# Product 1 of a two-level fast matrix product made joint over two pairs of tiles

## The chip, the core and the metric

The kernel runs on one core of a Trainium2 chip. The metric is the device time of one execution in microseconds; before the change it is 1103.38 us, the median of three runs. The engines are named PE (TensorE), DVE (VectorE), ACT (ScalarE), POOL (GpSimd) and SP (SyncE, which here issues all DMAs). Each has its own instruction queue and works it off in order.

## What is computed

The reference has a cross attention to a short memory and then a linear layer with a mixture of low-rank experts, each behind a layer norm and each added to x:

```python
x = x + xattn(layernorm(x), ctx_2048, mask)        # x: (8, 1024, 1024) float32, ctx: (8, 64, 1024)
x = x + ffn(layernorm(x), W, lora_A, lora_B, router_w)

# xattn: scores = h @ ctx.T / sqrt(D), masked, softmax, readout = attn @ ctx
# ffn:   base = h @ W.T                            # 1024 x 1024, all in float32
#        logits = h @ router_w.T ; top 2 of 8 experts, their softmax weights
#        expert_out = sum over experts of w_e * (h @ A_e.T) @ B_e.T * 2
```

## The kernel before

The 8192 rows are 64 tiles of 128 rows. Two tiles make a *pair* (tile r = 0 and r = 1), numbered u = 0 to 31; two pairs u and v = u + 1 make a *quad*. `first()` treats pairs 0 and 1, then `quad(u)` runs for u = 2, 4, ..., 30. Everything is laid out by hand: within `tc.manual_schedule` every engine executes its instructions in the order in which the Python code issues them, and an instruction waits on semaphores for what it reads and for what it overwrites. While a quad's linear layer runs, the attention of later pairs is threaded in between: in `quad(u)`, n and m (u + 2, u + 3) are the next quad's pairs, f and g (u + 4, u + 5) those of the one behind it.

**The linear layer.** For each pair, `h` (normalised rows) is turned on DVE into two halves of the contraction: `hA` (k = 0 to 3) and `hB` (k = 4 to 7), each 128 x 512 a tile (`rt_turn_tile`, line 557). To get there the rows go out to DRAM (`hd`) and come back blocked (`hs`). The 2 x 2 blocks (two tiles, two halves) are multiplied by the 2 x 2 blocks of W with Winograd's form of Strassen's scheme: seven products in place of eight. POOL makes the sums of the left side: `rt_sums` (line 629) makes s1, s2, s4 of a pair in three instructions of 128 x 512, and `rt_sum_3` (line 640) makes s3 in the place of `has[u][:, 1]`. Weights' sums `t1` to `t4` are made once in `first()`.

Products 2 to 7 are done *jointly* for the two pairs of a quad. `joint(i, u)` (line 788) takes the two pairs' 128-column operands as the rows of one more 2 x 2 scheme, so seven blocks of two 128 x 128 x 256 matmuls give what two products of four 128 x 128 x 512 matmuls gave. `joint_sums(i, u)` (line 774) makes that level's left sums on POOL in four instructions of 128 x 256; `quarter_sums` (line 680) made the weights' once. Inside `joint`, `to_x` brings quarter results from PSUM to where they are summed; block 5 (`block(chain, s2, q2, False)`, line 849) goes on accumulating in a bank whose first use must have been read, so PE waits there for that `to_x`. `hooks` give work of other stages that is issued behind step 1 to 7.

**Product 1** is not joint before. `product(u, 1)` (line 710) multiplies `has[u][:, 0]` by w11 into a bank `ch`; `one_add` (line 735) adds it to three of the pair's four output blocks, and much later `product(u, 8)` adds the low-rank term to the same bank and `product_add(u, 8)` takes it to the fourth. Product 6 goes to three of the output blocks as well: `joint(6, u)` puts it into `t_of(u)`, the place of `has[u][:, 0]` (free by then), and `six_add` (line 744) adds it to x on POOL.

**The start of a quad** (lines 1104 to 1216). On PE: product 1 of u, the last low-rank matmul of joint 4 of the quad before (`pending.pop()()`), the logits and low-rank matmuls `pa` of u (`rt_low_rank_tile`), product 1 of v with the turn `sc` of m's scores in it, `pa` of v with the turn `trw` of u's weighted low-rank part (`rt_turn_low_rank`), product 8, then readouts `ro`, scores `sct`, readouts, and joint 6. `trw` needs `rt_top(u)` (line 585): the top two experts' choice, some twenty short DVE instructions on the logits, of which several have both inputs in SBUF. On DVE `rt_top(u)` stands between the turn of v's tile 0 and that of v's tile 1; behind it come the turns `xT` of f and g for the attention, `att_divide`, `att_add(n)`, `rt_top(v)`, `att_add(m)`. On POOL: `rt_sums(u)` (already within joint 4 before, line 1295), `rt_sum_3(u)`, `rt_sums(v)`, `joint_sums(6)`, `rt_sum_3(v)`. On ACT: `x_sums(m)` of the attention's layer norm, which waits for `load_xt`, and the copy `axl` of the logits out of PSUM, with which `rt_top` begins. The order of the stages behind is joint 6, 2, 7, 3, 5, 4.

Of the kernel before, what the change touches and what calls it, by code (L numbers as in the profile page):

```python
# [14 lines left out]
ALU = mybir.AluOpType  # L15
# [9 lines left out]
def kernel(  # L25
# [520 lines left out]
    def hb_tile(u: int, r: int):  # L546
        if r == 0:
            h_tiles(u)
        t = turned.tile([P, KH, P], F32, tag="hB", name=f"hB_{u}_{r}", bufs=5)
        hbs[u].append(t)  # L550
        return t

    def rt_turn_pe(u: int, r: int):
        hb = hb_tile(u, r)
# [14 lines left out]
        for r in range(2):  # L569
            rt_low_rank_tile(u, r)  # L570

    def rt_low_rank_tile(u: int, r: int, midway=None):
        if r == 0:
            pas[u] = ps_rt.tile([P, 2, ER + E], F32, tag="rt", name=f"pa_{u}")
        pa = pas[u]
        for k in range(KD):
            h = has[u][:, r, k, :] if k < KH else hbs[u][r][:, k - KH, :]
            mm(pa[:, r, :], h, art_sb[:, k, :], start=(k == 0), stop=(k == KD - 1))  # L578
            if midway and k == KH:
                midway()  # L580
        if r == 1:
            axls[u] = small.tile([P, 2, ER + E], F32, tag="axl", name=f"axl_{u}", bufs=1)
            nc.scalar.copy(axls[u], pas.pop(u))

    def rt_top(u: int):

# [67 lines left out]
                by(o[:, k, :], x1[:, k, :], x2[:, k, :], op)  # L654


    quarters = {}

    def quarter(w, i: int, j: int):
        return w[:, i * HK : (i + 1) * HK, j * HH : (j + 1) * HH]  # L660
# [1 line left out]
    def quarter_sums_steps(name: str, w):  # L662

        by = nc.gpsimd.tensor_tensor
        b11, b12, b21, b22 = [quarter(w, i, j) for i in (0, 1) for j in (0, 1)]
        q2, q3, q4 = [
            const.tile([P, HK, HH], F32, name=f"{name}_{i}") for i in (2, 3, 4)
        ]
# [95 lines left out]
    def operand(i: int, p: int):  # L764

        if i in (2, 4):
            return hbs[p][i // 2 - 1]
        if i == 6:
            return sss[p]
        return {3: sms[p][:, 1], 5: sms[p][:, 0], 7: has[p][:, 1]}[i]  # L770
# [17 lines left out]
    def joint(i: int, u: int, hooks, final: bool = False, aside: bool = False):  # L788

# [11 lines left out]
        name = {2: "w21", 3: "w22", 4: "t4", 5: "t1", 6: "t2", 7: "t3"}[i]  # L801
        b11, b21, b22, q1, q2, q3, q4 = quarters[name]
        lower, upper = bank_of(f"jl{i}_{u}"), bank_of(f"ju{i}_{u}")
        p2, p5, p4, chain = [b[:, k * HH : (k + 1) * HH] for b in (upper, lower) for k in (0, 1)]

        def to_x(p, src, first: int, n: int):
            if i == 6:
                t = t_of(p)[:, first : first + n]
                if n == HH and (p == u and first == 0 or aside):
                    nc.scalar.copy(t, src)  # L810
# [85 lines left out]
    def first():  # L896
# [193 lines left out]

    pending = []

    def quad(u: int):

        v, n, m, f, g = [u + i for i in range(1, 6)]
# [5 lines left out]
        early = more and u == 2  # L1101
        late = more and u > 2

        product(u, 1, (lambda: att_sc(n)) if early else None, 1)
        if late:
            x_sums(m, (0,) if far else (0, 1))
            if not far:
                x_squares(m)
        if new_mem:
            mask_bias(b)  # L1110
        pending.pop()()
        if early:
            att_divide(n)
        one_add(u)
        rt_low_rank_tile(u, 0)
        if early:
            att_turn_p(n)
        rt_low_rank_tile(u, 1)
        if early:
            att_turn(m)  # L1120
        rt_turn_tile(v, 0)
        rt_top(u)
        rt_turn_tile(v, 1)
        if late:
            if far:
                x_sums(m, (1,))
                x_squares(m)
            x_root(m)
            product(v, 1, lambda: att_sc(m))
            if far:  # L1130
                att_turn_tile(f, 0)
                load_xs(g, (1,))
                att_turn_tile(f, 1)
            att_rstd(m)
            att_shift(m)
        rt_sum_3(u)
        rt_sums(v)
        if early:
            load_xs(f)
        elif far:  # L1140
            load_xt(f)
        if late:
            rt_low_rank_tile(v, 0)
            rt_turn_low_rank(u, bank_of(f"trw_{u}")[:, : 2 * P])
            att_exp(m)
            one_add(v, (0,))
        elif early:
            att_readout(n)
            att_scores(m)
            load_xs(g, (0,))  # L1150
            product(
                v, 1,
                {0: lambda: att_sc(m), 1: lambda: rt_turn_low_rank(u), 2: lambda: product(u, 8)},
            )
            att_rstd(m)
            att_exp(m)
            att_add(n)
            att_divide(m)
            f_sums(n)
            att_turn_tile(f, 0)  # L1160
            load_xs(g, (1,))
            load_xt(f)
            rt_low_rank_tile(v, 0)
            att_turn_tile(f, 1)
        else:
            product(v, 1)
            rt_low_rank_tile(v, 0)
            rt_turn_low_rank(u, bank_of(f"trw_{u}")[:, : 2 * P])
        if far:
            att_turn_tile(g, 0)  # L1170
        if late:
            att_divide(m)
        if far:
            att_turn_tile(g, 1)
        if late and not far:
            att_readout(n)
            att_add(n)
        rt_low_rank_tile(v, 1)
        if early or late and not far:
            att_turn_p(m, True)  # L1180
        if not early:
            product(u, 8)
        joint_sums(6, u)
        rt_sum_3(v)
        if late and far:
            att_readout(n)
            att_turn_p(m, True)
        product_add(u, 8)
        if late and far:
            att_add(n)  # L1190
# [5 lines left out]
        if far or not more:  # L1196
            rt_top(v)
        if more:
            att_readout(m)
        if late and not far:  # L1200
            att_add_tile(m, 0)
            rt_top(v)
        if late:
            f_sums(n)
        if new_mem:
            load_mem(b)
        if late and not far:
            att_add_tile(m, 1)
        elif more:
            att_add(m)  # L1210
        left_over = []
        if late:
            one_add(v, (1,))
            left_over.append(lambda: one_add(v, (2,)))
        else:
            one_add(v)

        hooks = {5: left_over, 7: []}
# [12 lines left out]
        def six():  # L1231
# [5 lines left out]
        if far:  # L1237
            x_stats(f)
            hooks[3].append(lambda: att_sc(f))
        if more:  # L1240
            hooks[3].append(lambda: f_rows(n))
        hooks[5] = []
# [49 lines left out]

        hooks = {1: [rows_0]}
        if more:
            hooks[3] = [lambda: rt_sums(n)]
        end_4 = joint(4, u, hooks, not more)

        def last():
            end_4()
# [55 lines left out]
```

## Time and profile before

| | |
|---|---|
| median of 3 runs | 1103.38 us (1103.31 to 1104.0) |
| profiled execution, span | 1101.5 us |
| granted TensorE clock | 1.00 |
| ACT busy | 556.2 us, 50% |
| matmul time of a whole product's piece, 128 x 512, mean of one | 593 ns (248 of them) |
| matmul time of a joint's piece, 128 x 256, mean of one | 385 ns (`ju` from w and s_j, 360) |
| DVE add from PSUM, 128 x 512 | 678 ns (124) |
| POOL sum, 128 x 512 / 128 x 256 | 1280 ns (31) / 731 ns (45) |
| DMA, mean over the span | 158 GB/s, 50.3% of 16 engines |

Each `mm` of float32 stands as two MATMUL instructions in the trace. A row of the timeline has the start in the span, the duration, the engine, the line, the operation with its tiles, and how many like it were joined; in square brackets stands the idle time before it and what ended it. Durations of matmuls include the drain of the array, which overlaps with the next one.

### The profile page before, as it was taken

What the parts mean: (1) busy time and instruction counts of PE and PEld (TensorE: products, weight loads), DVE (VectorE), ACT (ScalarE), POOL (GpSimd) and SP (SyncE); (2) the same over time, 40 slices, a digit from 0 to 9 for tenths busy, and PEclk for the clock granted to TensorE, in tenths of its full rate; (3) what the DMA queues carried; (4) which work ended last, traced back from release to release, by engine and by line L of the source; (5) the groups of instructions that cost most, each with busy time, mean ns of one, the idle gap of its engine ahead of it and who ended that gap; (6) DMA issues with size and microseconds to landing.
All of it is one profiled execution on the core that took longest, in us unless ns stands there. A gap on an engine that the chain in (4) does not pass through costs nothing.

```text
span 1101.5 us, 17562 instructions
## 1 busy us (share of the span) xinstructions
PE 1090.6 (99%) x5864; PEld 846.6 (77%) x5864; DVE 819.8 (74%) x2069; ACT 556.2 (50%) x1063; POOL 567.1 (51%) x629
## 2 busy tenths in 40 slices
PE   8999999999999999999999999999999999999998
PEld 6555787887878788787787878878787787877877
DVE  6666977769777687867869778687777778667665
ACT  4577363727539173573726638174472735636010
POOL 0079563635647265373644646356372644647372
PEclk9999999999999999999999999999999999999999
DMA  9857446363474625646265473635636355432301
GB/s 229 212 181 218 137 154 217 100 200 125 153 230 131 211 82 193 197 148 199 101 196 152 153 230 100 195 118 190 203 135 193 108 203 147 153 115 91 139 1 77
DMA packets 104921, 174.01 MB, mean 158 GB/s; under 512 B 12928, under 2 KB 77440, under 8 KB 104832
## 3 DMA queue, kind: packets, MB, share of 16 engines
q1 hardware_dynamic: 104832, 172.90, 50.3%
q8 instruction: 47, 0.77, 0.3%
q14 instruction: 42, 0.34, 0.1%
HBM read 107.84 MB, written 65.01 MB: 157 GB/s over the span
## 4 chain that ended last, share of the span: by engine, by line
PE 95%; DVE 2%; POOL 1%; ACT 1%; DMA 1%; SPq 0%; issue 0%; DVEq 0%; ACTq 0%; POOLq 0%
PE jl L703 28%; PE ju L703 21%; PE pa L578 10%; PE ch L703 9%; PE ro L480 5%; PE sct L412 5%; PE ju L695 4%; PE jl L695 3%; PE plain L703 3%; PE ch L695 2%; PE j L703 1%; DVE xT L89 1%; PE trw L621 1%; DMA xs<-in_x_dram 1%; PE ptp L466 1%; SPq L83 0%
## 5 line engine op out<-in xcount | busy, mean ns | idle before, releaser
L818 DVE TENSOR_TENSOR xt<-jl,xt 128x256 f32<-128x256 f32 x421 | 191.6, 485 | 139.6 <-PE jl L703 90.8
L818 DVE TENSOR_TENSOR xt<-ju,xt 128x256 f32<-128x256 f32 (+1 forms) x210 | 110.7, 551 | 56.2 <-PE ju L703 52.6
L635 POOL TENSOR_TENSOR s<-hA,hB 128x512 f32<-128x512 f32 x31 | 39.7, 1280 | 208.4 <-PE jl L703 92.9
L747 POOL TENSOR_TENSOR xt<-xt,hA 128x512 f32<-128x512 f32 x90 | 111.4, 1275 | 29.1 <-DVE hA L814 29.1
L195 ACT ACTIVATE junk<-xt 128x1024 uint8<-128x1024 f32 x60 | 63.2, 1053 | 123.6 <-DMA xt<-in_x_dram 123.1
L703 PE MATMUL ch<-w,hA 128*128 128x512 f32 x248 | 113.7, 593 | 0.0
L642 POOL TENSOR_TENSOR hA<-hA 128x512 f32<-128x512 f32 x31 | 39.6, 1277 | 139.8 <-PE pa L578 139.8
L703 PE MATMUL ju<-w,s_j 128*128 128x256 f32 x360 | 94.7, 385 | 0.2
L703 PE MATMUL ju<-t,s_j 128*128 128x256 f32 x360 | 92.7, 380 | 1.4 <-ACT hA L810 0.9
L692 DVE TENSOR_TENSOR xt<-ch,xt 128x512 f32<-128x512 f32 x124 | 81.3, 678 | 9.6 <-PE ch L703 4.5
L296 ACT ACTIVATE h<-xt,of_f 128x1024 f32<-128x1024 f32 x60 | 71.2, 1232 | 22.9 <-DVE of_f L292 14.1
L692 DVE TENSOR_TENSOR xt<-ro,xt 128x512 f32<-128x512 f32 x128 | 79.6, 676 | 3.7 <-PE ro L480 3.7
L703 PEld LDWEIGHTS ju<-t,s_j 128*128 128x128 f32 x360 | 66.2, 190 | 18.1 <-issue 5.3
L703 PEld LDWEIGHTS ch<-w,hA 128*128 128x128 f32 x248 | 44.7, 190 | 42.7 <-issue 41.8
L703 PE MATMUL jl<-t,s 128*128 128x256 f32 x300 | 76.0, 384 | 0.0
L703 PEld LDWEIGHTS ju<-w,s_j 128*128 128x128 f32 x360 | 63.9, 190 | 15.7 <-issue 6.8
L89 DVE STREAM_TRANSPOSE xT<-xs 128x1024 f32<-128x1024 f32 x60 | 73.6, 1229 | 0.6
L578 PEld LDWEIGHTS pa<-art_sb,hA 128*128 128x128 f32 x512 | 66.3, 190 | 9.8 <-issue 8.6
L578 PE MATMUL pa<-art_sb,hA 128*128 128x136 f32 x512 | 70.0, 280 | 0.0
L204 ACT ACTIVATE junk<-xt,of_x 128x1024 uint8<-128x1024 f32 x60 | 68.9, 1149 | 2.0
L578 PE MATMUL pa<-art_sb,hB 128*128 128x136 f32 x512 | 69.8, 279 | 0.0
L253 ACT ACTIVATE junk<-xt,of_f 128x1024 uint8<-128x1024 f32 x60 | 69.0, 1149 | 1.5
(202 smaller groups left out, 2425.0 us busy)
## 6 DMA issues: line engine op xcount, KB each, us to landing
xt<-in_x_dram SPq DMA_DIRECT2D x64, 512.0 KB, 4.8
out_dram<-xt SPq DMA_DIRECT2D x62, 512.0 KB, 3.0
xs<-in_x_dram SPq DMA_DIRECT2D x240, 128.0 KB, 4.1
hd<-h SPq DMA_DIRECT2D x60, 512.0 KB, 2.7
hs<-hd SPq DMA_DIRECT2D x240, 128.0 KB, 3.0
mem<-in_ctx_dram SPq DMA_DIRECT2D x16, 256.0 KB, 3.6
w<-in_w_t_dram SPq DMA_DIRECT2D x16, 256.0 KB, 10.0
ms<-in_ctx_dram SPq DMA_DIRECT2D x28, 64.0 KB, 2.0
```

Source lines behind the costliest of these rows:

```text
L89: nc.vector.transpose(dst.rearrange("p k (t i) -> p t k i", i=NB), src.rearrange("p t (k i) -> p t k i", i=NB),)
L195: nc.scalar.activation(nowhere, xts[u][r], AF.Identity, accum_out=sm[:, r, :])
L204: nc.scalar.activation(nowhere, xts[u][r], AF.Square, bias=nm[:, r, :], accum_out=ss[:, r, :],)
L253: nc.scalar.activation(nowhere, xts[u][r], AF.Square, bias=nm[:, r, :], accum_out=ss[:, r, :])
L296: nc.scalar.activation(h, xts[u][r], AF.Identity, bias=nmr[:, r, :], scale=rstd[:, r, :])
L412: mm(sct[r * M : (r + 1) * M, :], mt[:, k, :], x_ts[u][r][:, k, :], start=(k == 0), stop=(k == KD - 1),)
L578: mm(pa[:, r, :], h, art_sb[:, k, :], start=(k == 0), stop=(k == KD - 1))
L692: tt(xc, bank, xc, ALU.add)
L695: mm(bank, axwts[u][:, r, :], lb_sb[:, c0 : c0 + n], start=alone, stop=True, skip_group_check=True)
L703: mm(bank, a[:, k, :], w[:, k, :], start=(start and k == 0), stop=(k == n - 1), skip_group_check=True)
L747: nc.gpsimd.tensor_tensor(xc, xc, t_of(u), ALU.add)
L818: tt(xc, src, xc, ALU.add)
```

## The change

From the third quad (u = 4) on, product 1 is done by `joint(1, u)` too, behind the logits of both pairs. Its four quarter results go into `t_of(u)`, which is the place of its own left operand `has[u][:, 0]`; joint 6 then adds to what is there. All sums that read `has[u][:, 0]` come before the first copy into that place. `zero_add` adds product 1 alone to block (0, 0) on POOL before joint 6, and `six_add` later adds both to the other three. The low-rank term of block (1, 1) gets a bank of its own (`lora_alone`). The weights' quarter sums of w11 share one SBUF place with those of t1: both sets are written to DRAM once, and each quad loads w11's (`load_pieces` in joint 4, step 1, of the quad before) and t1's (in joint 2, step 3). In `first()`, `quarter_sums` and `keep_pieces` of w11 stand behind `plain(1, 0, 0)`, `keep_pieces` of t1 behind `t1_two()`. The places of `hB` are now assigned by hand, so that the fifth is spare for joint 1's s3. Quad 2 keeps the old order (`quad_start`).

```diff
+    def shared_pieces(name: str):
+        kept[name, "tile"] = sums.tile([P, 3, HK, HH], F32, tag="q", name=f"q_{name}")
+        return [kept[name, "tile"][:, i] for i in range(3)]
+    def keep_pieces(name: str):
+        kept[name] = dram.tile([P, 3, HK, HH], F32, tag=f"q_{name}", name=f"qd_{name}", bufs=1)
+        nc.sync.dma_start(out=kept[name], in_=kept[name, "tile"])
+    def load_pieces(name: str):
+        quarters[name] = *quarters[name][:4], *shared_pieces(name)
+        nc.sync.dma_start(out=kept[name, "tile"], in_=kept[name])
...
+    def zero_add(u: int):
+        xc = xts[u][0][:, :HB]
+        nc.gpsimd.tensor_tensor(xc, xc, t_of(u), ALU.add)
+
+    def lora_alone(u: int):
+        bank = bank_of(f"lo_{u}")
+        lora(u, bank, 1, HB, HB, True)
+        pps[u] = None, bank
...
         s3 = lo[:, :HK]
+        if i == 1:
+            s3 = turned.tile(
+                [P, KH, P], F32, tag=f"hB{spare_place(u)}", name=f"s3_{u}", bufs=1
+            )[:, :HK]
...
         def to_x(p, src, first: int, n: int):
-            if i == 6:
+            if i in (1, 6):
                 t = t_of(p)[:, first : first + n]
-                if n == HH and (p == u and first == 0 or aside):
+                if fresh and n == HH and p == u and first == (HH if i == 1 else 0):
                     nc.scalar.copy(t, src)
-                elif n == HH:
+                elif fresh and n == HH:
                     nc.vector.tensor_copy(t, src)
                 else:
                     tt(t, src, t, ALU.add)
...
+        quarter_sums("w11", w11)
+        keep_pieces("w11")
...
+        keep_pieces("t1")
...
+    def quad_joint_start(u: int):
...
+        if new_mem:
+            mask_bias(f // PPB)
+        rt_sums(u)
+        rt_low_rank_tile(u, 0)
+        rt_turn_tile(v, 1)
+        rt_sums(v)
+        pending.pop()()
+        if more:
+            x_sums(m, (0,))
+        rt_low_rank_tile(u, 1)
+        rt_top(u)
+        if more:
+            x_sums(m, (1,))
+            x_squares(m)
+        if far:
+            att_turn_tile(f, 0)
+            load_xs(g, (1,))
+            att_turn_tile(f, 1)
+            load_xt(f)
+        pa_v = bank_of(f"pa_{v}")
+        rt_low_rank_tile(v, 0, pa_v, False)
+        rt_low_rank_tile(v, 1, pa_v, False)
+        rt_sum_3(u)
+        rt_sum_3(v)
+        joint_sums(6, u)
+
+        hooks = {}
+        if more:
+            hooks[1] = [lambda: att_sc(m)]
+        def low_rank():
+            rt_turn_low_rank(u)
+            rt_low_rank_copy(v)
+            if more:
+                x_root(m)
+        def shift():
+            att_rstd(m)
+            att_shift(m)
+        hooks[2] = [low_rank]
+        if more:
+            hooks[4] = [shift]
+        end_1 = joint(1, u, hooks, fresh=True)
+        if more:
+            att_exp(m)
+        end_1()
+        for p in (u, v):
+            zero_add(p)
+        lora_alone(u)
+        if more:
+            att_divide(m)
+        if far:
+            att_turn_tile(g, 0)
+            att_turn_tile(g, 1)
+        if more:
+            att_readout(n)
+            att_turn_p(m, True)
+        product_add(u, 8)
+        if more:
+            att_add(n)
...
-        end_6 = joint(6, u, hooks, aside=not more)
+        end_6 = joint(6, u, hooks, fresh=not as_joint)
...
         def low_v():
-            product(v, 8)
+            if as_joint:
+                lora_alone(v)
+            else:
+                product(v, 8)
             product_add(v, 8)
...
+        if as_joint:
+            hooks[3].append(lambda: load_pieces("t1"))
...
         def rows_0():
+            if more:
+                load_pieces("w11")
             end_5()
...
         if more:
-            hooks[3] = [lambda: rt_sums(n)]
+            hooks[5] = [lambda: rt_turn_tile(m, 0)]
         end_4 = joint(4, u, hooks, not more)
+        if more:
+            joint_sums(1, n)
```

The quads from u = 4 on call `quad_joint_start(u)` and no longer issue `product(u, 1)`, `product(v, 1)`, `one_add` of either, or `rt_sums` of the next pair in joint 4. `quad_start` of quad 2 also makes `quarter_sum("w11")`, one POOL instruction, ahead of `joint_sums(6, 2)`.

More of the change, by code (lines that the diff above doesn't have):

```diff
@@ L548, in hb_tile, with place_of, spare_place @@
             h_tiles(u)
-        t = turned.tile([P, KH, P], F32, tag="hB", name=f"hB_{u}_{r}", bufs=5)
+        t = turned.tile(
+            [P, KH, P], F32, tag=f"hB{place_of(u, r)}", name=f"hB_{u}_{r}", bufs=1
+        )
         hbs[u].append(t)
         return t
+    places = {(u, r): (2 * u + r) % 5 for u in range(4) for r in range(2)}
+    def place_of(u: int, r: int):
+        if (u, r) not in places:
+            a, b, c, d = [places[p, k] for p in (u // 2 * 2 - 2, u // 2 * 2 - 1) for k in (0, 1)]
+            w = u // 2 * 2
+            places.update({(w, 0): a, (w, 1): c, (w + 1, 0): b, (w + 1, 1): d})
+        return places[u, r]
+    def spare_place(u: int):
+        used = {places[p, k] for p in (u, u + 1) for k in (0, 1)}
+        return ({0, 1, 2, 3, 4} - used).pop()
     def rt_turn_pe(u: int, r: int):
@@ L570, in rt_low_rank, with rt_low_rank_tile @@
             rt_low_rank_tile(u, r)
-    def rt_low_rank_tile(u: int, r: int, midway=None):
-        if r == 0:
+    def rt_low_rank_tile(u: int, r: int, bank=None, copy: bool = True):
+        if r == 0 and bank is not None:
+            pas[u] = bank[:, : 2 * (ER + E)].rearrange("p (r c) -> p r c", r=2)
+        elif r == 0:
             pas[u] = ps_rt.tile([P, 2, ER + E], F32, tag="rt", name=f"pa_{u}")
@@ L578, in rt_low_rank_tile, with rt_low_rank_copy @@
             mm(pa[:, r, :], h, art_sb[:, k, :], start=(k == 0), stop=(k == KD - 1))
[L579 to L583, printed above, removed]
+        if r == 1 and copy:
+            rt_low_rank_copy(u)
+    def rt_low_rank_copy(u: int):
+        axls[u] = small.tile([P, 2, ER + E], F32, tag="axl", name=f"axl_{u}", bufs=1)
+        nc.scalar.copy(axls[u], pas.pop(u))
     def rt_top(u: int):
@@ L654, in weight_sums @@
                 by(o[:, k, :], x1[:, k, :], x2[:, k, :], op)
-    quarters = {}
+    quarters, kept = {}, {}
+    SHARED = ("w11", "t1")
+    def shared_pieces(name: str):
[7 more added lines that the diff above has]
+        nc.sync.dma_start(out=kept[name, "tile"], in_=kept[name])
     def quarter(w, i: int, j: int):
@@ L665, in quarter_sums_steps @@
         b11, b12, b21, b22 = [quarter(w, i, j) for i in (0, 1) for j in (0, 1)]
-        q2, q3, q4 = [
-            const.tile([P, HK, HH], F32, name=f"{name}_{i}") for i in (2, 3, 4)
-        ]
+        if name in SHARED:
+            pieces = shared_pieces(name)
+        else:
+            pieces = [const.tile([P, HK, HH], F32, name=f"{name}_{i}") for i in (2, 3, 4)]
+        q2, q3, q4 = pieces
         quarters[name] = b11, b21, b22, b12, q2, q3, q4
@@ L769, in operand @@
             return sss[p]
-        return {3: sms[p][:, 1], 5: sms[p][:, 0], 7: has[p][:, 1]}[i]
+        if i in (1, 7):
+            return has[p][:, i // 7]
+        return {3: sms[p][:, 1], 5: sms[p][:, 0]}[i]
     jss = {}
@@ L786, in joint_sums, with joint @@
         jss[i] = s1, s2, s3, s4
-    def joint(i: int, u: int, hooks, final: bool = False, aside: bool = False):
+    def joint(i: int, u: int, hooks, final: bool = False, fresh: bool = False):
         v = u + 1
@@ L800, in joint @@
         s1, s2, s3, s4 = jss.pop(i)
-        name = {2: "w21", 3: "w22", 4: "t4", 5: "t1", 6: "t2", 7: "t3"}[i]
+        name = {1: "w11", 2: "w21", 3: "w22", 4: "t4", 5: "t1", 6: "t2", 7: "t3"}[i]
         b11, b21, b22, q1, q2, q3, q4 = quarters[name]
@@ L1091, with quad_start @@
     pending = []
+    def quad_start(u: int):
+        v, n, m, f, g = [u + i for i in range(1, 6)]
+        more, far = n < NP, f < NP
+        new_mem = far and f % PPB == 0
+        product(u, 1, lambda: att_sc(n), 1)
+        if new_mem:
+            mask_bias(f // PPB)
+        pending.pop()()
+        att_divide(n)
+        one_add(u)
+        rt_low_rank_tile(u, 0)
+        att_turn_p(n)
+        rt_low_rank_tile(u, 1)
+        att_turn(m)
+        rt_turn_tile(v, 0)
+        rt_top(u)
+        rt_turn_tile(v, 1)
+        rt_sum_3(u)
+        rt_sums(v)
+        load_xs(f)
+        att_readout(n)
+        att_scores(m)
+        load_xs(g, (0,))
+        product(
+            v, 1,
+            {0: lambda: att_sc(m), 1: lambda: rt_turn_low_rank(u), 2: lambda: product(u, 8)},
+        )
+        att_rstd(m)
+        att_exp(m)
+        att_add(n)
+        att_divide(m)
+        f_sums(n)
+        att_turn_tile(f, 0)
+        load_xs(g, (1,))
+        load_xt(f)
+        rt_low_rank_tile(v, 0)
+        att_turn_tile(f, 1)
+        att_turn_tile(g, 0)
+        att_turn_tile(g, 1)
+        rt_low_rank_tile(v, 1)
+        att_turn_p(m, True)
+        quarter_sum("w11")
+        joint_sums(6, u)
+        rt_sum_3(v)
+        product_add(u, 8)
@@ new lines, in quad_joint_start @@
+    def quad_joint_start(u: int):
+        v, n, m, f, g = [u + i for i in range(1, 6)]
+        more, far = n < NP, f < NP
+        new_mem = far and f % PPB == 0
+        next_mem = f + 2 < NP and (f + 2) % PPB == 0
+        if new_mem:
+            mask_bias(f // PPB)
+        rt_sums(u)
+        rt_low_rank_tile(u, 0)
+        rt_turn_tile(v, 1)
+        rt_sums(v)
+        pending.pop()()
+        if more:
+            x_sums(m, (0,))
+        rt_low_rank_tile(u, 1)
+        rt_top(u)
+        if more:
+            x_sums(m, (1,))
+            x_squares(m)
+        if far:
+            att_turn_tile(f, 0)
+            load_xs(g, (1,))
+            att_turn_tile(f, 1)
+            load_xt(f)
+        pa_v = bank_of(f"pa_{v}")
+        rt_low_rank_tile(v, 0, pa_v, False)
+        rt_low_rank_tile(v, 1, pa_v, False)
+        rt_sum_3(u)
+        rt_sum_3(v)
+        joint_sums(6, u)
+        hooks = {}
[7 more added lines that the diff above has]
+        def shift():
+            att_rstd(m)
+            att_shift(m)
[4 more added lines that the diff above has]
+        if more:
+            att_exp(m)
+        end_1()
[3 more added lines that the diff above has]
+        if more:
+            att_divide(m)
+        if far:
+            att_turn_tile(g, 0)
+            att_turn_tile(g, 1)
+        if more:
+            att_readout(n)
+            att_turn_p(m, True)
+        product_add(u, 8)
+        if more:
+            att_add(n)
@@ L1100, in quad @@
         next_mem = f + 2 < NP and (f + 2) % PPB == 0
[L1101 to L1164, printed above, removed]
-        else:
-            product(v, 1)
-            rt_low_rank_tile(v, 0)
-            rt_turn_low_rank(u, bank_of(f"trw_{u}")[:, : 2 * P])
@@ L1169, in quad @@
[L1169 to L1187, printed above, removed]
@@ L1188, in quad @@
-        product_add(u, 8)
-        if late and far:
-            att_add(n)
+        as_joint = u > 2
+        if as_joint:
+            quad_joint_start(u)
+        else:
+            quad_start(u)
         if far:
@@ L1195, in quad @@
             load_ms((f + 2) // PPB)
-        if far or not more:
-            rt_top(v)
+        rt_top(v)
         if more:
             att_readout(m)
[L1200 to L1203, printed above, removed]
+        if as_joint and more:
             f_sums(n)
@@ L1206, in quad @@
             load_mem(b)
-        if late and not far:
-            att_add_tile(m, 1)
-        elif more:
+        if more:
             att_add(m)
[L1211 to L1215, printed above, removed]
+        if not as_joint:
             one_add(v)
-        hooks = {5: left_over, 7: []}
+        hooks = {5: [], 7: []}
         hooks[5 if more else 7].append(lambda: rt_turn_low_rank(v))
@@ L1223, in quad @@
             hooks[5].append(lambda: turn_mem((f + 2) // PPB))
-        end_6 = joint(6, u, hooks, aside=not more)
+        end_6 = joint(6, u, hooks, fresh=not as_joint)
         joint_sums(2, u)
         def low_v():
-            product(v, 8)
+            if as_joint:
+                lora_alone(v)
+            else:
+                product(v, 8)
             product_add(v, 8)
@@ L1239, in quad @@
             hooks[3].append(lambda: att_sc(f))
+        if as_joint:
+            hooks[3].append(lambda: load_pieces("t1"))
         if more:
@@ L1294, in quad @@
         if more:
-            hooks[3] = [lambda: rt_sums(n)]
+            hooks[5] = [lambda: rt_turn_tile(m, 0)]
         end_4 = joint(4, u, hooks, not more)
+        if more:
+            joint_sums(1, n)
         def last():
```

## The prediction

> **What bounds the kernel now.** I read the busy shares and the chain of waits first.
>
> ```profile
> PE 1090.6 (99%) x5864; PEld 846.6 (77%) x5864; DVE 819.8 (74%) x2069; ACT 556.2 (50%) x1063; POOL 567.1 (51%) x629
> ...
> PE 95%; DVE 2%; POOL 1%; ACT 1%; DMA 1%; SPq 0%; issue 0%; DVEq 0%; ACTq 0%; POOLq 0%
> ```
>
> PE is full and makes 95% of the chain: a microsecond it loses or saves is one of the kernel. Next PE's timeline in the quad u = 8 (start, duration, row):
>
> ```profile
> 308.08 3.60 PE L703 MATMUL ch<-w,hA 128*128 128x512 f32 x8
> 311.51 0.59 PE L695 MATMUL jl<-lb_sb,axwt 128*128 128x256 f32 x2
> ...
> 334.51 1.03 PE L703 MATMUL ju<-t,s_j 128*128 128x256 f32 x4
> 335.37 1.03 PE L703 MATMUL jl<-t,s_j 128*128 128x256 f32 x4
> ```
>
> Ends are modelled, so I take start to start: a whole product 1 costs 3.43 us, a block of a joint 0.86. From quad to quad (308.08, 374.65, 441.27) it is 66.6 us, and no PE row from 308 to 341 notes idle time. Third, POOL in the same quad:
>
> ```profile
> 320.20 1.28 POOL L635 TENSOR_TENSOR s<-hA,hB 128x512 f32<-128x512 f32 x1 [3.96 <-DVE hB L89]
> 321.55 1.28 POOL L636 TENSOR_TENSOR s<-s,hA 128x512 f32<-128x512 f32 x1
> ...
> 327.13 1.28 POOL L642 TENSOR_TENSOR hA<-hA 128x512 f32<-128x512 f32 x1
> ```
>
> POOL waits 3.96 us ahead of rt_sums(v), since the turn of v's second tile stands behind rt_top(u) on DVE; rt_sums then takes 3.93 us (to 324.13) and joint_sums 3.00 (to 327.13). Fourth, DVE there: rt_top(u), the two turns of f, rt_top(v), att_add(m).
>
> ```profile
> 316.27 0.24 DVE L591 MAX8 top<-axl 128x8 f32<-128x8 f32 x2 [0.43 <-ACT axl L583]
> ...
> 320.04 2.48 DVE L89 STREAM_TRANSPOSE xT<-xs 128x1024 f32<-128x1024 f32 x2
> ...
> 332.40 2.48 DVE L692 TENSOR_TENSOR xt<-ro,xt 128x512 f32<-128x512 f32 x4
> ```
>
> Last, the final quad of before, the one place where POOL is busy during an rt_top:
>
> ```profile
> 1054.60 0.23 DVE L591 MAX8 top<-axl 128x8 f32<-128x8 f32 x2
> ...
> 1058.76 0.37 ACT L810 COPY hA<-ju 128x256 f32<-128x256 f32 x1 [2.61 <-POOL hA L642]
> 1058.80 0.65 DVE L609 TENSOR_TENSOR we<-we,we 128x16 f32<-128x16 f32 x1
> ...
> 1059.18 1.13 PE L703 MATMUL ju<-t,s_j 128*128 128x256 f32 x4 [0.92 <-ACT hA L810]
> ...
> 1060.42 1.87 DVE L692 TENSOR_TENSOR xt<-ch,xt 128x512 f32<-128x512 f32 x3
> ```
>
> Two things matter. A copy into hA waits for POOL's rt_sum_3, which reads hA, and PE waits for the copy. And rt_top runs from 1054.60 to 1060.5: 5.9 us, against 2.6 in nearly every other. Its sums with both inputs in SBUF end just behind POOL's instructions (L609 at 1059.45, POOL's at 1059.41; 0.65 us where the quiet median is 0.17). L457 says the same: 0.29 us 16 times beside an idle POOL, 0.51 to 1.01 us 16 times beside a busy one. Adds from PSUM (0.68) and turns (1.23 a tile) do not change.
>
> **The change, part by part.** *PE's work.* Two products of 3.43 go, seven blocks of 0.86 come: 6.86 - 6.05 = -0.81 us a quad, 14 quads, -11.4. Logits, turns, readouts, scores and low-rank matmuls stay in number.
>
> *DVE and POOL work.* one_add's six adds (0.60 each, start to start) go; two copies of 0.34, a third behind the last block, and two adds of 0.60 come, and joint 6's one ACT copy becomes a DVE add. POOL gains joint_sums(1), 3.00, and two zero_add of 1.23. Totals are no problem; places are. Let T be time from the end of joint 4's last block (308.08).
>
> *PE, unhindered:* pa of u and end_4's lora to 4.14 (1.85 + 0.43 + 1.85), pa of v to 7.85, joint 1: block, sc (0.11), block to 9.69; there stands the turn of u's weights, trw, which needs rt_top(u); 0.22 and two blocks to 11.64, where block 5 needs the copy of u's first quarter; end at 14.23.
>
> *POOL:* joint_sums(1) starts when v's first tile is turned, behind joint 4's fifth block: DVE's add 306.12 to 306.54, the turn to 307.2, so T - 0.8. Then rt_sums(u) from 2.2, rt_sums(v) from 6.1, rt_sum_3(u) 10.0 to 11.3, rt_sum_3(v) to 12.5: no gap, since hB of v is turned by 2.5, ahead of rt_top. The cover which rt_top(u) had, POOL's 3.96 us of waiting, is gone.
>
> *rt_top(u):* pa ends at 4.14, ACT's copy at 4.75 (316.27 was 0.43 behind such a wait), rt_top starts at 4.8. By the quiet row it takes 2.6; by the final quad 5.9; at most it lasts till POOL's run is over, 13.1. I take 13.1: the nearest row, the final quad, needed seven POOL ends from first to last, most of them of 0.73 us instructions; here the ends lie 1.2 to 1.35 apart (6.15, 7.4, 8.7, 10.1, 11.3, 12.5), and the last two sums run behind them. So trw waits 13.15 - 9.69 = 3.46 us. Behind rt_top on DVE stand the two turns of f (2.4) and only then the copy (0.42): 15.84, where PE, through trw and two blocks, wants it at 15.10: 0.80 more. Joint 1 ends at 18.5, 4.26 late. At the quiet row these would be POOL's own waits, 0.24 and 0.36.
>
> *From there (E) to joint 6.* Before, block 5 of joint 6 came 12.25 us behind the last lora of this stretch (323.12 to 335.37). DVE now has in a row: 0.20 to see the bank; a copy and two adds 1.54; att_divide, which meets a zero_add on POOL, 1.1 (quiet 0.55); two turns of g 2.4; an add 0.60; att_add(n) 2.4; rt_top(v) 2.52, POOL idle; att_add(m) 2.4; the add into hA 0.42, which block 5 needs and which ACT did before: 13.57. So 1.32 us more (quiet 0.85). Per quad 4.26 + 1.32 - 0.81 = +4.77, for the 12 quads u = 4 to 26: +57.2. u = 28 and 30 have no turns of f: 3.46 in joint 1, some 2.4 and 2.0 ahead of joint 6, less 0.81 and less the stalls that are there today (2.0 and 1.1): +3.0 and +3.5.
>
> *DMA, SP and the first quads.* Each quad loads two sets of pieces, 0.79 MB each. 512 KB landed in 4.8 us, so at most 7.4; w11's starts when joint 5 ends (T - 7.3) and is wanted at 7.85. On SP two stores, xt of g, xs of f stand behind it; the DMA engines idled from 298 to 303, so these slip by 0 to 2.2 us. Then xt lands by T + 3.3 (1.05 before), its sum on ACT, ahead of the axl copy, ends by 4.5: +0.2, which POOL's ends swallow. t1's set leaves behind joint 1 and has 20 us. Of the sums of w11 (3 x 1.27) POOL's wait of 55.5 us hides all; quarter_sum("w11"), 1.28, falls in quad 2, where POOL is 9 us ahead. The two stores at the start: 0 to +1. Cost taken: 0.
>
> Sum: 57.2 + 6.5 = +63.7. The profiled execution spans 1101.5, 1.9 under the median of 1103.4: **1167 us**.
>
> The Trainium skill (SBUF — State Buffer, Who interferes with whom) calls the read port that DVE's second SBUF input shares with GpSimd an exclusive lock for a whole instruction. That speaks against this change: by the rule each such sum of rt_top waits out an instruction of 1.28 us, about 1167; by the bare row of 5.9 us the sum would be 1134.
>
> **The rivals.** *B, rt_top(u) takes 5.9 as it stands in the final quad* (its sums find gaps between POOL's instructions: these exist between dependent ones, 0.07 us). It ends at 10.7, trw waits 1.04, the copy behind the turns 0.80; 1.84 + 1.32 - 0.81 = +2.35 a quad, 12 of them and 1.0 and 1.1 at the end: 1134. *C, no meeting at all:* 0.60 + 0.85 - 0.81 = +0.64, and -0.7 in the last two: 1110. Against it stand all 16 busy rows of L457. *D, faster:* the copies and rt_top come in time and PE saves its 0.81 fourteen times: 1092. Its place is block 5 of joint 1 and of joint 6; it decides where the waits there stay under 0.81 together, for which rt_top(u) must be quiet and POOL 0.6 us ahead. Against it: POOL's sums alone, with no gap, end at 12.5. *E, longer waits slow PE itself:* the first 16 matmuls of 128 columns took 3.78 us (0.24 each), later ones 0.11; if gaps of 3.5 us bring that back for as long again, 1.7 us a quad: 1188. No gap past 1.1 us stands in this trace behind the start, so nothing shows it. The Trainium skill (TensorE: Matmul & The Clock Gate, What's actually happening) gives an idle window of about 3.4 us, its clock then halved, which is an estimate for E too.
>
> **How the numbers follow.** The forecast 0.67, B 0.16, C 0.07, D 0.05, E 0.05. The range goes from under B to 1182, which leaves out C, D and most of E: 1130 to 1182. Two tenths of a percent, 2.2 us, is what a measurement here can tell from none. Faster 0.05 (D), same 0.01, slower 0.94.
>
> **What would show it.** After: in each joint quad rt_top(u) of about 8 us (L611 to L632), trw's load waiting about 3.5 us for DVE axl, PE's block 5 of joint 1 waiting for DVE's copy into hA, and that of joint 6 for DVE's add; quads of 71.4 us; PE's busy share near 93%. Wrong it is if rt_top(u) stays near 2.6, or if POOL's run ends earlier than T + 12.

## The result, and the profile after

The changed kernel takes **1185.62 us** (median of 4 runs, 1182.97 to 1187.12) against 1103.51 us for the kernel before beside it (1103.31 to 1104.0): 1.0741 times as long, 95% interval 1.0726 to 1.0757. The forecast was 1167 us in a range of 1130 to 1182: the direction holds, the size is 18 to 19 us short. The profiled execution spans 1184.1 us, against the forecast's 1101.5 + 63.7 = 1165.2.

The page of the changed kernel: the busy shares, and the chain of waits.

```profile
PE 1114.6 (94%) x6032; PEld 894.5 (76%) x6032; DVE 899.9 (76%) x2072; ACT 558.7 (47%) x1060; POOL 645.8 (55%) x717
...
PE 68%; DVE 23%; DMA 5%; issue 2%; SPq 1%; ACT 1%; DVEq 0%
```

PE's part of the chain fell from 95% to 68% and DVE's rose from 2% to 23%. PE's busy time rose by 24 us although the change takes 0.81 us of work from each of 14 quads: PE ran slower for part of the time. DVE's rose by 80 us: operations that wait inside an instruction count as busy.

DVE in the quad u = 8 of the changed kernel, where joint 4 ends at T = 320.48 (start, duration, row, idle time before it):

```profile
325.24 0.24 DVE L611 MAX8 top<-axl 128x8 f32<-128x8 f32 x2 [0.73 <-ACT axl L603]
325.51 1.10 DVE L614 TENSOR_TENSOR of_top<-top 128x2 f32<-128x2 f32 x1
...
326.93 0.92 DVE L619 CAST of_top<-idx 128x4 f32<-128x4 uint32 x1
327.88 1.34 DVE L623 TENSOR_TENSOR we<-iota_e,of_top 128x16 f32<-128x16 f32 x2
...
331.84 1.19 DVE L629 TENSOR_TENSOR we<-we,we 128x16 f32<-128x16 f32 x1
333.06 0.49 DVE L632 TENSOR_TENSOR axl<-axl,we 128x128 f32<-128x128 f32 x2
333.47 2.52 DVE L89 STREAM_TRANSPOSE xT<-xs 128x1024 f32<-128x1024 f32 x2
```

POOL beside it:

```profile
325.33 1.27 POOL L657 TENSOR_TENSOR s<-hB,s 128x512 f32<-128x512 f32 x1
326.55 1.27 POOL L655 TENSOR_TENSOR s<-hA,hB 128x512 f32<-128x512 f32 x1
...
330.50 2.49 POOL L662 TENSOR_TENSOR hA<-hA 128x512 f32<-128x512 f32 x2
```

rt_top(u) runs from T + 4.8 to T + 13.1 and takes 8.3 us, where rt_top(v), with POOL idle, takes 2.6. L614 ends at 326.61, as POOL's L657 does (326.60); the CAST of L619 ends at 327.85 against 327.82 for L655. In all, six of its operations end so, each 0.02 to 0.04 us behind one of six POOL instructions in a row.

PE in the same quad, and PE's busy time and granted clock in three stretches of it (stretch, length, busy time and rows, clock, the DMA engines' share, GB/s):

```profile
329.30 1.03 PE L741 MATMUL jl<-w,hA 128*128 128x256 f32 x4
333.50 0.66 PE L641 MATMUL trw<-ident,axl 128*128 128x128 f32 x2 [3.17 <-DVE axl L632]
333.95 1.91 PE L741 MATMUL ju<-w,hA 128*128 128x256 f32 x4
335.65 1.62 PE L741 MATMUL ju<-w,s_j 128*128 128x256 f32 x4
337.11 1.03 PE L741 MATMUL jl<-q_w,s_j 128*128 128x256 f32 x4
...
339.70 1.02 PE L733 MATMUL lo<-lb_sb,axwt 128*128 128x512 f32 x2
...
353.34 1.13 PE L741 MATMUL jl<-t,s_j 128*128 128x256 f32 x4 [0.70 <-DVE hA L869]
```

```profile
329.00:333.40 4.40, 1.33 (x7) 1.00 0.99 304
333.40:336.90 3.50, 3.40 (x10) 0.51 1.02 288
336.90:341.00 4.10, 4.10 (x18) 1.00 0.60 225
```

PE stands 3.2 us before trw. **Then its clock is 0.51 for the next stretch**, and a block of a joint takes 1.70 us (333.95 to 335.65) where 0.86 is usual. In the records of the clock such a stretch of half clock is 3.41 us long, twice 6.8 us, and follows trw's wait in 13 of the 14 quads. In the last quad, u = 30, trw's wait is 3.27 us and the clock stays at 1.00 behind it; there it halves behind a later wait, at joint 6 (1.03 us for four pieces behind the first wait, 2.07 behind the second):

```profile
1128.04 1.03 PE L741 MATMUL ju<-w,s_j 128*128 128x256 f32 x4
...
1139.19 2.07 PE L741 MATMUL jl<-t,s_j 128*128 128x256 f32 x4 [3.23 <-DVE hA L869]
```

### The profile page after: what moved, and what is told of

Read it like the earlier page. It is cut to its first block, busy times and chain, and to the rows that moved or that the text cites. A ratio compares the mean times of both kernels' runs of the same rounds, so it can differ in the third digit from the quotient of the medians.

```text
span 1184.1 us, 18090 instructions
## 1 busy us (share of the span) xinstructions
PE 1114.6 (94%) x6032; PEld 894.5 (76%) x6032; DVE 899.9 (76%) x2072; ACT 558.7 (47%) x1060; POOL 645.8 (55%) x717
## 4 chain that ended last, share of the span: by engine, by line
PE 68%; DVE 23%; DMA 5%; issue 2%; SPq 1%; ACT 1%; DVEq 0%
PE jl L741 26%; PE ju L741 22%; DVE xt L730 6%; PE pa L597 5%; PE ju L733 3%; PE jl L733 3%; DVE xT L89 3%; DVE we L623 2%; DVE hA L869 2%; PE plain L741 2%; DMA xs<-in_x_dram 2%; DVE we L628 2%; DVE we L629 2%; PE ch L741 1%; DVE of_top L614 1%
## 5 line engine op out<-in xcount | busy, mean ns | idle before, releaser
L195 ACT ACTIVATE junk<-xt 128x1024 uint8<-128x1024 f32 x60 | 63.3, 1055 | 157.2 <-DMA xt<-in_x_dram 156.5
L741 PE MATMUL ju<-w,s_j 128*128 128x256 f32 x472 | 133.2, 408 | 0.2
L837 POOL TENSOR_TENSOR s_j<-hA 128x256 f32<-128x256 f32 x29 | 21.2, 730 | 180.1 <-DVE hA L89 180.1
L741 PEld LDWEIGHTS ju<-w,s_j 128*128 128x128 f32 x472 | 92.3, 206 | 22.7 <-issue 7.4
L837 POOL TENSOR_TENSOR s_j<-hB 128x256 f32<-128x256 f32 x30 | 21.8, 728 | 101.6 <-PE ju L741 101.6
L837 POOL TENSOR_TENSOR s_j<-s 128x256 f32<-128x256 f32 x45 | 32.7, 726 | 74.0 <-PE jl L741 74.0
L597 PEld LDWEIGHTS pa<-art_sb,hB 128*128 128x128 f32 x512 | 64.0, 190 | 0.0
L243 ACT ACTIVATE junk<-xt 128x1024 uint8<-128x1024 f32 x60 | 63.2, 1053 | 1.9 <-DVE xt L730 0.4
L741 PE MATMUL jl<-w,s 128*128 128x256 f32 x240 | 61.6, 379 | 0.0
```

The lines of the kernel that those rows point to most:

```text
L195: nc.scalar.activation(nowhere, xts[u][r], AF.Identity, accum_out=sm[:, r, :])
L741: mm(bank, a[:, k, :], w[:, k, :], start=(start and k == 0), stop=(k == n - 1), skip_group_check=True)
```

## The experiments

Unless an edit is said to stand on another kernel, it is an edit of the changed kernel. "Quads" are means over the 12 from u = 4 to 26, from the first `pa` of one to that of the next; they are 66.50 us before the change and 72.40 after it.

### Is the lock enough by itself? (e3, on the kernel before)

```
+        if late:
+            rt_sum_3(u)
+            idle_sums(v, 5)      # 5 sums hB + hB of 128x512 on POOL
         rt_top(u)
...
-        rt_sum_3(u)
+        if not late:
+            rt_sum_3(u)
```

> The kernel before with five idle POOL sums of 128 x 512 (into a place that is overwritten afterwards) put into POOL's wait of 3.96 us, under rt_top(u), in the quads u = 4 to 28. Theory 1: rt_top(u) goes from 2.6 to 6.5 to 7.5 us, trw waits about 2 us, and DVE, full from there to joint 6, brings all of it to PE: some 4 us a quad, 1145 to 1165 us, clock 1.00 as each wait stays under 3.4 us. Rival (a busy POOL does not matter to DVE; rt_sums(v) only starts 2.4 us later, and joint 6 needs it 8 us later): 1103 to 1106 us.

Measured: 1146.91 us against 1104.04, ratio 1.039 (1.0373 to 1.0407); quads of 69.89. DVE, then the waits (engine, line, cause: total, times, longest), of this kernel:

```profile
323.79 0.72 DVE L594 TENSOR_TENSOR of_top<-top 128x2 f32<-128x2 f32 x1
...
324.83 0.81 DVE L599 CAST of_top<-idx 128x4 f32<-128x4 uint32 x1
```

```profile
PE ptp L466 <- DVE s L457: 19.4, 13, 1.5
...
PE trw L621 <- DVE axl L612: 12.3, 13, 1.0
```

Work that nobody waits for, on an engine with time to spare, costs 43 us. rt_top(u) takes 6.03 us. The wait at trw is only 1.0 us of the 3.4 a quad, less than was expected. The largest part, 1.5 us a quad, is PE's wait ahead of ptp, the turn of m's softmax, for the division in att_divide: DVE's later work is late. At joint 6's fifth block PE waits no more, but it gets there 3.4 us late (26.8 us after the first `pa`, 23.4 before).

### Take the lock away (e2)

rt_top(u) with one operand of each sum in spare columns of the PSUM bank of `pa_u`, so that no sum reads two operands from SBUF:

```
-        rt_top(u)
+        rt_top_aside(u)
...
+        first_of, w1, w2 = [pairs[:, i] for i in range(3)]     # PSUM
+        idf = pairs[:, 3:].rearrange("p a b o -> p (a o) b")   # PSUM
+        nc.vector.tensor_copy(first_of, top[:, :, 0:1])
+        tt(dl, top[:, :, 1:2], first_of, ALU.subtract)
...
+        tt(both[:, 0], we2, w2.to_broadcast([P, 2, E]), ALU.mult)
+        tt(both[:, 1], we, both[:, 0], ALU.add)
```

> The changed kernel with rt_top(u) of the joint quads rewritten so that none of its DVE sums reads both inputs from SBUF: one of each pair lies in spare columns of the PSUM bank of the logits. Same result, two more short instructions. Theory 1 (rt_top(u) waits out POOL's instructions because of its second SBUF input): rt_top(u) 2.6 to 3.4 us in place of 8.3, no wait at trw, clock 1.00, block 5 and 6 of joint 1 wait 0.2 and 0.4 us for POOL's sums, joint 6's block 5 some 13.1 to 13.6 us behind the low-rank matmul: 1107 to 1120 us. Rival (rt_top(u) is slow from late inputs or from PE): 1180 to 1188 us.

Measured: 1129.26 us, ratio 1.0225 (1.0203 to 1.0246); quads of 68.19, granted clock 0.998. So the lock and what follows from it are some 56 us of the 82. PE reaches trw at T + 9.68, where 9.69 was worked out for a PE without hindrance. But the time is 10 us above the expected range. DVE in the quad u = 8 (T = 313.08):

```profile
318.38 0.16 DVE L651 TENSOR_TENSOR of_top<-top,pa 128x2 f32<-128x2 f32 x1
...
318.85 0.17 DVE L655 CAST pa<-idx 128x4 f32<-128x4 uint32 x1
...
319.22 1.23 DVE L660 TENSOR_SCALAR of_top<-of_top 128x2 f32<-128x2 f32 x1
...
323.72 1.25 DVE L89 STREAM_TRANSPOSE xT<-xs 128x1024 f32<-128x1024 f32 x1 [0.55 <-DMA xs<-in_x_dram]
...
325.63 0.43 DVE L903 COPY hA<-ju 128x256 f32<-128x256 f32 x1 [0.36 <-POOL hA L698]
```

The sum of L651 and the CAST of L655 are down to 0.16 and 0.17 us while POOL is as busy as in the changed kernel. Three waits stand behind them: a TENSOR_SCALAR that still takes 1.23 us, a turn of f that waits for its rows, and copies into hA that wait for POOL to have read hA. The ladder below takes them one by one.

### Keep PE at work during the wait (e1_warm, e1_half)

```
+        for _ in range(warm):
+            mm(trw[:, 0, :], ident, ident, start=True, stop=True)
         for r in range(2):
             nc.tensor.transpose(trw[:, r, :], axl[:, r, :ER], ident)
...
-            rt_turn_low_rank(u)
+            rt_turn_low_rank(u, warm=12)      # e1_half: 6
```

> The changed kernel with 12 dummy matmuls (128 x 128 identity, 0.22 us each, 2.6 us together) issued on PE just ahead of the turn trw of u's weights, so that PE is not idle while it waits for rt_top(u). Nothing else moves. Theory 1 (the wait of 3.3 us is DVE's, and what exceeds the forecast is PE at half speed for 3.4 us behind it): trw still at 13.0 us from the quad's first pa, rt_top(u) still 8.3 us, but the granted clock 1.00 in place of 0.977 and quads of 71.4 in place of 72.3 us: 1170 to 1176 us. Rival (the excess lies in DVE or DMA): no change, 1184 to 1188 us.

Measured: 1175.3 us, ratio 1.0645 (1.0627 to 1.0663), clock 0.997; quads of 71.54 against 72.40.

> The changed kernel with 6 dummy matmuls in front of trw instead of e1's 12, so that about 0.65 us of the gap of 3.3 us is filled instead of 1.3 and 2.65 us are left. If the clock falls only behind gaps near 3.3 us: as e1, clock 0.995 or more, 1174 to 1177. If it falls from a shorter gap on: clock under 0.985, 1180 to 1187.

Measured: 1176.79 us, ratio 1.066 (1.0643 to 1.0676), clock 0.999; quads of 71.54. The waits of e1_warm, then of e1_half:

```profile
PE jl L743 <- DVE hA L869: 8.2, 12, 0.7
...
PE trw L643 <- DVE axl L632: 6.0, 14, 0.5
```

```profile
PE trw L643 <- DVE axl L632: 24.9, 14, 1.9
```

The clock is 10 us of the result. The dummies fill more than I reckoned: e1_half leaves a gap of 1.9 us, not 2.65, and after 1.9 us the clock stays up. The row of L869 is the forecast's copy behind the turns of f, 0.7 us in each of the 12 quads. In the changed kernel it is not seen: PE, at half clock, reaches that block only when the copy is done (337.11 above, the copy ended at 336.30). Of the 1.7 us that half clock takes from PE in 3.41 us, some 0.8 lie over this wait, which is how 0.86 a quad come out.

### POOL's order alone (e4)

```
-        rt_sums(u)
+        rt_sums(u, False)      # its last sum, s4, left out
...
         rt_sum_3(u)
+        rt_sums(v, False)
         rt_sum_3(v)
+        rt_sum_4(u)
+        rt_sum_4(v)
```

> The changed kernel with only POOL's order altered: the two s4 sums, which do not read the place that joint 1 writes, come behind rt_sum_3 of u and v. POOL's run is as long as before, but hA may be written from T + 10.1 in place of 12.5. Theory 1 (rt_top(u) lasts as long as POOL's run, and the copies stand behind it and the turns of f on DVE): no change, 1182 to 1188 us, rt_top(u) 8.3 us. Rival (POOL's late sums hold the copies up): 1165 to 1178 us.

Measured: 1179.29 us, ratio 1.0695 (1.0674 to 1.0717); quads of 71.80. Between the two: trw comes at T + 12.80 instead of 13.02, and PE still waits 3.0 us there in each quad, with half clock behind it in 13 of the 14. As long as rt_top(u) lasts to the end of POOL's run, the order inside the run is worth 0.2 us; the rest of the 0.6 us a quad is put down to the clock, from the rows and not from a run of its own: no quad here has the double stretch of half clock that two quads of the changed kernel have, and elsewhere the low-rank matmul behind joint 1 starts 18.7 to 19.1 us after T instead of 19.0 to 19.4.

### What e2 has left: a ladder (e5 to e9), and the lock put back (e10)

Each kernel of the ladder stands on the one before it, e5 on e2.

e5, the load of the pieces behind the stores on SP's queue:

```
         def rows_0():
-            if more:
-                load_pieces("w11")
             end_5()
             for p in (u, v):
                 store(p, 0)
...
+            if more:
+                load_pieces("w11")
```

> The kernel of e2 with the load of product 1's pieces behind the two stores of the quad on SP's queue, where it was ahead of them. In e2 the turn of f's second tile waits 0.55 to 1.7 us for its rows in 11 quads, since SP holds the stores, the load of g's rows and the loads of f's rows behind the pieces' load until joint 5 has let go of the pieces' place. My theory: this queue is a part of what e2 has over the 1110 forecast for a change without the lock; rows come some 4 us earlier, the wait for them goes, the copy behind them is bound by POOL's rt_sum_3 instead: 1112 to 1121. The rival, that these waits lie beside others: 1125 to 1131 as e2.

e6, the sum of 1.0 into PSUM:

```
-        dl, e2, d1 = [of_top[:, i] for i in range(3)]
-        first_of, w1, w2 = [pairs[:, i] for i in range(3)]
+        dl, e2 = [of_top[:, i] for i in range(2)]
+        first_of, w1, w2, d1 = [pairs[:, i] for i in range(4)]
```

> e5 with one more operation of rt_top(u) moved off SBUF: the sum of e2 and 1.0, one SBUF operand in and one SBUF result, now writes PSUM. In e2 it took 1.23 us in the midst of POOL's run where it takes 0.16 in rt_top(v). My theory: an operation of this kind too waits for POOL although it reads one operand; it goes back to 0.16 and rt_top(u) from 4.1 to 3.0 us; of this little shows, since the copy waits for POOL anyway: 0 to 5 us under e5. The rival: the 1.23 us is the wait for ACT's exponential, and stays 1.2.

e7 adds e4's order of POOL.

> e6 with POOL's s4 sums of both pairs behind the two sums of rt_sum_3, as in e4. The copies into hA may write only when rt_sum_3 has read hA; both sums of it come 1.25 to 2.5 us earlier. My theory: the copies then come in time, 2 to 9 us under e6, 1100 to 1113. The rival, that the copies are bound by the turns of f on DVE: within 2 us of e6.

e8, the second turn of f behind joint 1's first copy:

```
             att_turn_tile(f, 0)
             load_xs(g, (1,))
-            att_turn_tile(f, 1)
-            load_xt(f)
...
+        def second_turn():
+            att_turn_tile(f, 1)
+            load_xt(f)
         hooks[2] = [low_rank]
+        if far:
+            hooks[2].append(second_turn)
```

> e7 with the turn of f's second tile behind the first copy of joint 1 on DVE instead of ahead of it. My theory: joint 1 then has no wait on DVE, but DVE has the same work to do until joint 6's fifth block and stays about 0.85 us late there, what the change saves of PE's work: 0 to 4 us under e7, 1098 to 1109, so no less than the kernel before or only just. The rival, that DVE's order leaves joint 6 in time as well: 1091 to 1097, under the kernel before.

| kernel | us | ratio, 95% interval | quads, us |
|---|---|---|---|
| e2 | 1129.26 | 1.0225, 1.0203 to 1.0246 | 68.19 |
| e5 | 1124.1 | 1.0189, 1.0167 to 1.0211 | 67.70 |
| e6 | 1122.35 | 1.0173, 1.0152 to 1.0195 | 67.64 |
| e7 | 1119.12 | 1.0137, 1.0112 to 1.0162 | 67.42 |
| e8 | 1115.51 | 1.0103, 1.0086 to 1.012 | 67.16 |
| e11 | 1106.52 | 1.0023, 1.0014 to 1.0032 | 66.41 |
| e9 | 1096.34 | 0.9937, 0.9923 to 0.995 | 65.76 |

(The last two rows belong to experiments told below.) Neighbours from e2 to e8 lie within each other's intervals or touch them; the waits tell the steps apart better than the times. These are the waits of PE's weight load for joint 1's fifth block on the copy, and of the copies on POOL (engine, line, cause: total, times, longest), first in e2, then in e5, then in e7:

```profile
PEld jl L777 <- DVE hA L903: 14.4, 14, 2.0
```

```profile
DVE hA L903 <- POOL hA L698: 14.5, 15, 2.4
...
PEld jl L777 <- DVE hA L903: 7.5, 14, 1.3
```

```profile
PEld jl L782 <- DVE hA L908: 4.1, 7, 0.8
...
DVE hA L908 <- POOL hA L703: 1.8, 1, 1.8
```

From e2 to e5 PE's wait falls from 14.4 to 7.5 us, and the copies wait for POOL instead, 14.5 us in all; with e7's order that wait is gone but for one; in e8 PE's has no row left among the 60 longest. e6 did what was expected: its TENSOR_SCALAR takes 0.16 us in place of 1.23 and little shows in the time. e5 came 3 us above its range; the times of e7 and e8 came 6 us above theirs, though each step was about as large as expected, 3.2 and 3.6 us.

Two things about the rows of f were not as expected. The stores leave SP at T - 5.8 in e2 and in e5 alike, so the load ahead of them does not hold them there: beside it they land 5.1 us after that, without it 2.7, and the loads behind them wait for that landing. And the turns' wait for their rows, 9.5 us over the kernel in e2, falls to 1.7 in e5 but is back at 6.6 in e6 and 7.8 in e7, where the turns come earlier; in e8 it is 0.9.

What e8 still loses, as expected, is joint 6, 0.86 us a quad at its fifth block; beside it 0.33 go in the scores of g and 0.19 ahead of ptp, which wait for DVE too and had not been counted.

e9, two edits of DVE's work between the joints:

```
-            att_divide(m)
+            att_divide_aside(m)      # the reciprocals in ptp's PSUM bank
...
-            att_add(m)
+            att_add_tile(m, 0)
...
+            if as_joint:
+                hooks[2].insert(0, lambda: att_add_tile(m, 1))
```

> e8 with two edits on DVE between joint 1 and joint 6: att_divide's reciprocals in PSUM, so that the division no longer waits for POOL's zero_add (0.98 us there, 0.55 quiet), and the second half of att_add(m) behind joint 6's first add into hA instead of ahead of it. In e8's steady quads PE loses 0.86 us at joint 6's fifth block, 0.33 in the scores of g and 0.19 ahead of ptp, all waiting for DVE. My theory: these 1.4 us are all that is left of the change's cost and mostly go: quads of 65.8 to 66.2 us against 67.2, 1098 to 1105, about the kernel before. The rival, that the wait moves to block 6 or to joint 2: 1110 to 1117.

Measured: 1096.34 us (1095.23 to 1097.43), 0.9937 of the kernel before, a little under the expected range. **It is faster than both kernels**, 0.6% under the one before. PE and DVE in the same quad, first e8's wait and division, then e9's:

```profile
404.78 1.13 PE L782 MATMUL jl<-t,s_j 128*128 128x256 f32 x4 [0.70 <-DVE hA L910]
```

```profile
393.07 0.98 DVE L457 TENSOR_TENSOR s<-s,of_s 128x128 f32<-128x128 f32 x1
```

```profile
398.86 1.03 PE L794 MATMUL ju<-t,s_j 128*128 128x256 f32 x4
399.72 1.03 PE L794 MATMUL jl<-t,s_j 128*128 128x256 f32 x4
```

```profile
389.41 0.29 DVE L467 TENSOR_TENSOR s<-s,ptp 128x128 f32<-128x128 f32 x1
```

In e9 block follows block at 0.86 us, and the division takes 0.29 us beside a busy POOL.

e11 has the moved adds alone, without the division in PSUM:

> e9 without its division in PSUM: only the second half of att_add(m) stands behind joint 6's first add. In e8's steady quads 0.86 us are lost at joint 6's fifth block and 0.33 and 0.19 ahead of it. My theory: the moved adds take away the 0.86 alone, and the division, which waits for POOL's zero_add, keeps the 0.5 us at the scores of g and at ptp: quads of 66.2 to 66.4 us, 1101 to 1106. The rival, that the division makes little of it since DVE's time there is covered once the adds are moved: as e9, under 1098.

Measured: 1106.52 us (1103.93 to 1107.42, 11 runs), ratio 1.0023 (1.0014 to 1.0032); quads of 66.41. By the quads the moved adds are worth 0.75 us and the division 0.65. In e11 the fifth block of joint 6 follows the fourth without a wait, but starts 26.99 us after T where it starts at 26.47 in e9: the 0.5 us ahead of it are the division's. Its times are half a microsecond above the range; in its profiled execution quad 4 starts 2.0 us later than in e9, behind a stretch of half clock in the start. So with the moved adds alone the kernel does not pass the one before; the division alone was not tried.

e10 is e9 with rt_top(u) in SBUF again:

> e9 with rt_top(u) as in the changed kernel, its operands in SBUF; all other edits of e5 to e9 stay. My theory: the lock is the head of the chain, PE waits at trw for 3.1 us again and its clock falls behind each wait, but the copies and joint 6 come in time now: 1147 to 1168. The rival, that the order of the other work was the larger part: under 1130.

Measured: 1155.67 us, ratio 1.0471 (1.0455 to 1.0487), 59 us over e9. PE in two quads, one after the other:

```profile
399.93 0.44 PE L689 MATMUL trw<-ident,axl 128*128 128x128 f32 x2 [2.96 <-DVE axl L646]
400.21 1.50 PE L794 MATMUL ju<-w,hA 128*128 128x256 f32 x4
401.50 1.91 PE L794 MATMUL ju<-w,s_j 128*128 128x256 f32 x4
```

```profile
470.64 0.44 PE L689 MATMUL trw<-ident,axl 128*128 128x128 f32 x2 [2.96 <-DVE axl L646]
470.92 1.03 PE L794 MATMUL ju<-w,hA 128*128 128x256 f32 x4
471.79 1.03 PE L794 MATMUL ju<-w,s_j 128*128 128x256 f32 x4
```

The wait is the same, 2.96 us; behind the first the clock is halved, behind the second it is not. In the first the low-rank matmul after joint 1 starts 19.09 us after T, in the second 17.68: with no copy to wait for, a halved stretch costs 1.4 us. The lock with its wait of 3 us is the head of the loss whatever the order of the work around it.

## Why the prediction was wrong in its size, step by step

- *PE's work, -0.81 us a quad*: right. In e9, where hardly anything waits, joint 1 ends at T + 14.22 (14.23 was worked out) and quads are 0.74 us shorter than before the change.
- *POOL's run without a gap to T + 12.5, rt_top(u) to 13.1, trw's wait of 3.46*: right. POOL's last sum ends at 332.99, T + 12.5; trw comes at T + 13.02, 3.34 late. Rival B falls with it, since no gap in POOL's run let rt_top through sooner. (The final quad was not the only place before where POOL worked during an rt_top: the one at 994.62, with two POOL sums in it, took 3.17.)
- *The copy behind two turns of f, 0.80*: right in its place, 0.7 in e1_warm, but hidden in the changed kernel behind a slower PE.
- *DVE's chain to joint 6's fifth block, 13.57*: right; 13.64, from the low-rank matmul at 339.70 to the block at 353.34.
- *DMA and SP, "these slip by 0 to 2.2 us", cost 0*: about right. From the end of joint 4 the stores leave at T - 5.8 before and after; beside the pieces' load they land 5.4 us after that in place of 2.7, and what waits for the landing starts later: the loads of f's rows at T + 1.3 instead of T - 1.0, 2.3 us. In the changed kernel it costs nothing, since the turns of f are behind rt_top(u), at T + 13. With that cover gone, in e2, the turns wait for the rows up to 1.7 us.
- **The step that failed: "No gap past 1.1 us stands in this trace behind the start, so nothing shows it", the price of nothing for PE's clock, and 0.05 for rival E.** The forecast itself put a wait of 3.46 us into every quad, so its own trace could not be like the one before. The clock does fall behind it, in 13 of the 14 quads. e1_warm, with a shorter gap, shows what it is worth: 0.86 us in each of the 12 quads. Rival E had the cause but 1.7 us a quad for it; that its 1188 lies near the measured time is luck, since other terms make up the difference.
- *Rival C's quiet 0.85 ahead of joint 6*: 0.77 by its own terms (13.57 less 0.55 less 12.25), which is 1 us of its 1110.
- *u = 28 and u = 30, +3.0 and +3.5*: mis-sized, +4.37 and +6.7. With e1_warm u = 28 is +3.02, so there it was the clock. In u = 30 rt_top(v) meets POOL (4.98 us), PE waits 3.4 us at joint 6 where 2.0 was taken, and the clock is halved behind that wait, though not behind trw's.

The difference of 18.9 us in the spans is thus 13.5 in 12 quads (5.90 against 4.77 us each, of which 0.86 is the clock), 1.4 in u = 28, 3.2 in u = 30 and 0.8 in the start. The last quad's split between its wait and its clock is read from its rows, not tried.

## What to carry to other kernels

When a forecast puts a new wait on the engine that is the bound, price what the engine does after such a wait too: the trace of before can't show it, and the wait's length, with the place where it falls on the clock's grid (below), says what it costs. Ask of each engine pair that shares something what its long instructions do to a chain of short ones: a chain that takes 2.6 us beside an idle POOL took 8.3 beside a POOL without a gap, and one operand of each sum in PSUM gave most of it back. And a cost that is hidden behind a larger one comes out when the larger one is mended: without the lock the change stood at 1.0225 of the time before, and only the steps of the ladder, down to 0.5 us in a division, brought it to 0.9937.

## What the runs showed of the hardware

- DVE's operations that end only with POOL's instruction are not the sums of two SBUF operands alone: a CAST (0.17 us quiet, 0.92 in the changed kernel) and a TENSOR_SCALAR (0.16, 1.23 in e2), each with one operand, do it as well, and no longer once one end lies in PSUM (0.17 in e2, 0.16 in e6). The Trainium skill (SBUF — State Buffer, Who interferes with whom) says of such operations that they can take the shared port in a mode of two ports; these rows agree.
- The halved stretches in the steady quads of the changed kernel start 21 or 22 times 3.413 us apart, those of e10 mostly 41 times, two quads. So the clock goes by a grid of its own, and where a gap lies on the grid decides, not its length alone: trw's gaps of 3.0 us halve the clock in 13 of 14 quads of e4 and those of 3.2 us in 13 of the changed kernel, but not the 3.27 us in its last; in e10 a gap of 2.96 us halves it in the quad u = 10 and one of 3.36 us, in u = 8, does not; those of 1.9 us never do in e1_half. Lay the grid of 3.413 us over each trace and add up PE's idle time in each step (by the ends of its rows, which are modelled): behind the start, over all 14 traces, the clock is halved after each of the 45 steps with 2.03 us or more, and from full clock after none with 1.96 or less. The gap of 3.27 us lies on two steps, with 1.70 and 1.57. 21 steps are 71.7 us, nearly a quad of the changed kernel, which is why its gaps meet the grid in much the same way each time. The Trainium skill (TensorE: Matmul & The Clock Gate, What's actually happening) tells of a free-running window of 3413 ns after which an idle PE is at half clock; the stretches and their grid agree, and a gap somewhat shorter than the window was enough.
